# A graph layer, causal attention and eight experts on one core: pools split, roots and denominators moved, one branch at the end

## The chip, the core and the metric

The kernel runs on one core of one Trainium2 chip. A core has a matrix engine (PE), a vector engine (DVE), a scalar engine (ACT), a general engine (POOL, or GpSimd) and a queue engine for transfers (SP). Matmul results go to PSUM, eight banks of 2 KB a partition, from which DVE and ACT read them; the rest lies in SBUF. Each engine takes its instructions in the order in which they were written; across engines they wait on semaphores. The metric is the device time of one launch in microseconds, lower is better. Two kernels that differ by more than 0.2% can be told apart by several runs.

## What is computed

The input is 4096 tokens of 256 numbers and a 4096 x 4096 adjacency matrix, all in 32-bit floats. Cut to what matters:

```python
# layer 0: graph part
f = layernorm(x)
h = adj @ (f @ neigh_W.T) / (adj.sum(1) + 1)
x = x + concat([f, h]) @ lin_W.T
# attention and experts, on y = layernorm(x)
h = rmsnorm(y);  q, k, v = h @ wq.T, h @ wk.T, h @ wv.T     # 4 query heads, 2 key heads of 64
q, k = rope(q), rope(k)
att = softmax(causal(q @ k.T / 8));  z = y + (att @ v) @ wo.T
t = rmsnorm(z);  probs = softmax(t @ router_w.T)             # 8 experts, the best 2 are kept
out = z + sum over the two experts of weight * (silu(t @ w1.T) * (t @ w3.T)) @ w2.T
x = x + out
```

## The kernel before, in words

A planner is not used: instructions go to each engine in the order of the Python text. The line numbers are those of the kernel before.

**Graph part.** Tokens lie in 8 blocks of 512, and the adjacency matrix in 8 x 8 blocks. `aggregate(b, steps)` forms one block row: for each `jb` it multiplies by a seven-product (Strassen) scheme, line 412, 28 matmuls in all, each of which the profile records twice; after the seventh of 14 pairs it calls the steps that belong to that `jb` (lines 419 to 421). The sums that the scheme needs are made by `halve(n)` on DVE, four additions (lines 366 to 369), one of them into `kT`. `halve` of the next block stands at the top of each round (line 401). Row 0 has as its steps `features` (matmuls `pf`, line 377; ACT copies, line 382; DVE additions, line 385; four subtractions for `g`, lines 389 to 392), `turned_x` (transposes on PE, line 312) and `normed_x` (statistics on DVE, inverse root on POOL, lines 158 and 159, normalizing on DVE, line 167). Rows 1 to 7 have `qkv(b-1)`: `norm` at `jb` 0, then transposes, projections (line 179) and rotation. At the end of a row, lines 432 to 448 combine the seven products on ACT and DVE, up to `deg` (lines 440 to 442). In PSUM the part has two banks for `tr`, two for `pj` and four for `acc`, these from one pool of four buffers.

**Attention.** Runs of four key tiles, `runs`, follow each other: blocks in the order 3, 0, 4, 1, 5, 2, 6, 7, two head pairs each. A run has its scores (line 537; PE), exponentials (line 542; ACT, into `pt`), sums over keys (line 560; DVE) and products with the values (line 572; PE). The scores use one pool of three buffers of two banks each, `a_sc`; products have one bank, and everything else shares one bank, `ms`. In step n the order is: sums of the first tiles of run n, scores of run n+1, place 2n, the other sums, products of run n, place 2n+1. A place is where one piece of other work is put: `normalize` (denominators: `dn`, lines 585 to 591, with a DVE reciprocal), the output projection, routing, the writes of the rows into the experts' lists, the last block's projections, and a check of the scores' size, `guard`. `at` hands out places, one piece that uses PE at each.

**Experts.** Groups of 256 or 128 rows of one expert: `load_rows`, `load13` and `load2` on SP, `prepare` (transposes, line 1057), `hidden` (line 1078), `combine` (products, line 1123; scaling by the gate on DVE, line 1134; an indirect transfer that adds rows to the output, line 1151, on POOL). The score buffers hold `hidden`'s results. `combine` of group k-1 follows `hidden` of group k.

**The end.** After the last group every engine loads `rest_flag` and branches (lines 1258 and 1259) past four groups that are rarely needed; then every engine loads `flag` and branches (lines 1812 and 1813) past a general kernel for scores that are too large. With these inputs neither is taken. A drain and a barrier follow (line 1884).

Of the kernel before, what the change touches and what calls it, by code (L numbers as in the profile page):

```python
# [1 line left out]

# [6 lines left out]
F32 = mybir.dt.float32  # L9
# [7 lines left out]
P = 128  # L17
# [48 lines left out]
def fast_kernel(  # L66
# [13 lines left out]
    cos: bass.AP,  # L80
    sin: bass.AP,
    out: bass.AP,
    flag: bass.AP,
):


    nc = tc.nc
# [124 lines left out]
    with (  # L212
# [2 lines left out]
        tc.tile_pool(name="gx", bufs=2) as gx,  # L215
        tc.tile_pool(name="g_tr", bufs=2, space=PSUM) as p_tr,
        tc.tile_pool(name="g_pj", bufs=2, space=PSUM) as p_pj,
        tc.tile_pool(name="g_acc", bufs=4, space=PSUM) as p_acc,
    ):
        blocks = {}  # L220

# [102 lines left out]

        inputs, turned = {}, {}

        def normed_x(b):
            stats(gx, b)
            power(rstd[b], mv[b][:, :, 1:2], 1.0, EPS_LN)
            inputs[b] = gx.tile([P, TB, C], F32, tag="f", name=f"f_{b}", bufs=1)  # L330
            for t in range(TB):
                normed(inputs[b][:, t, :], b, t, rstd[b][:, t])
            nc.gpsimd.memset(g[b][:, G22 : T1 + 1, :, HC : HC + 1], 1.0)

        def turned_x(b):
            turned[b] = qT[b % 4]
# [35 lines left out]
        def features(b):  # L372
            fT = turned.pop(b)
            for t in range(TB):
                pj = p_pj.tile([P, 512], F32, tag="pj", name=f"pf_{b}_{t}")
                for c in range(2):
                    nc.tensor.matmul(
                        pj, fT[:, c, t * P : (t + 1) * P], ml_sb[:, c, :],
                        start=(c == 0), stop=(c == 1),
                    )  # L380
                i = t // 2 * 2
                nc.scalar.copy(
                    g[b][:, i : i + 2, t % 2, 0:HC], pj[:, 0:C].rearrange("p (h c) -> p h c", h=2)
                )
                nc.vector.tensor_add(res[b][:, t, :], res[b][:, t, :], pj[:, C : 2 * C])
                if b == 0 and t == 1:
                    halve(0)
            part = [g[b][:, k, :, 0:HC] for k in range(7)]
            nc.vector.tensor_sub(part[T1], part[G12], part[G11])
            nc.vector.tensor_sub(part[T3], part[G22], part[G12])  # L390
            nc.vector.tensor_sub(part[T2], part[G22], part[T1])
            nc.vector.tensor_sub(part[T4], part[T2], part[G21])

        def aggregate(b, steps):

            acc = [
                [p_acc.tile([P, 512], F32, tag="acc", name=f"acc_{b}_{t}_{k}") for k in range(2)]
                for t in range(2)
            ]
            for jb in range(NB):  # L400
                halve(b * NB + jb + 1)
                m = halves_of.pop(b * NB + jb)
                order = [(p, t) for p in PRODUCTS for t in range(2)]
                if jb == 0 and b:
                    load_tables(b - 1)
                if jb == NB - 1 or b and jb == 0:
                    order = [(p, t) for t in range(2) for p in PRODUCTS]
                for i, ((number, left, right), t) in enumerate(order):
                    bank, at, w = AT[number]
                    for k in range(2):  # L410

                        nc.tensor.matmul(  # L412
                            acc[t][bank][:, at : at + w], m[left][:, k, t * P : (t + 1) * P],
                            g[jb][:, right, k, 0:w],
                            start=(jb == 0 and k == 0 and number in (1, 3)),
                            stop=(jb == NB - 1 and k == 1),
                            skip_group_check=True,
                        )
                    if i == 6:
                        for step in steps.get(jb, ()):  # L420
                            step()
                load(b * NB + jb + 3)
# [27 lines left out]
        def qkv(b):  # L450

            made = {}

            def norm():
                stats(gx, b)
                var = mv[b][:, :, 1:2]
                power(rstd[b], var, 1.0, EPS_LN)
                power(both[b], var, *BOTH)
                made["h0"] = gx.tile([P, TB, C], F32, tag="f", name=f"h0_{b}", bufs=1)
                for t in range(TB):  # L460
                    normed(made["h0"][:, t, :], b, t, both[b][:, t])
# [18 lines left out]
            def turn_heads(t):  # L480
# [1 line left out]
                heads(b, t, made.pop(t), tr)  # L482

            return {
                0: [norm], 2: [turn], 3: [lambda: rotate(0)], 4: [lambda: rotate(1)],
                5: [lambda: turn_heads(0), lambda: rotate(2)],
                6: [lambda: turn_heads(1), lambda: rotate(3)],
                7: [lambda: turn_heads(2), lambda: turn_heads(3)],
            }


        normed_x(0)
        fold()
        load(2)
        for b in range(6, NB):
            load_x(b)
        turned_x(0)
        normed_x(1)
        features(0)
        turned_x(1)  # L500
        normed_x(2)
        steps = {
            jb: [
                lambda f=f, b=jb + k: f(b)
                for f, k in ((features, 1), (turned_x, 2), (normed_x, 3)) if jb + k < NB
            ]
            for jb in range(NB)
        }
        steps[3].append(load_rest)
        aggregate(0, steps)  # L510
        for b in range(1, NB):
# [5 lines left out]
    with (  # L517
# [1 line left out]
        tc.tile_pool(name="ex", bufs=2) as ex,  # L519
        tc.tile_pool(name="sp", bufs=9) as sp,  # L520
        tc.tile_pool(name="ax", bufs=2) as ax,
        tc.tile_pool(name="a_sc", bufs=3, space=PSUM) as p_sc,
        tc.tile_pool(name="a_y", bufs=1, space=PSUM) as p_y,
        tc.tile_pool(name="a_ms", bufs=1, space=PSUM) as p_ms,
    ):
        probs, sums, accs, ys, flats, chosen, squares, picks = ({} for _ in range(8))
        puts = []

        def scores(b, p, s):
# [1 line left out]
            sb, i = divmod(s, TB)  # L531
            off = i * P if sb == b else 0
            w = 512 - off
            ps = p_sc.tile([P, 2, 512], F32, tag="sc", name=f"sc_{b}_{p}_{s}")
            for j in range(2):
                hd = slice(j * HD, (j + 1) * HD)
                nc.tensor.matmul(  # L537
# [314 lines left out]
            ]  # L852


        def guard():
            six = {}

# [6 lines left out]
            def second():  # L864
# [9 lines left out]
                most = ax.tile([1, 1], F32, tag="most", name="most", bufs=1)  # L874
                nc.vector.tensor_reduce(most, qk2.rearrange("o p j -> o (p j)"), AX.X, ALU.max)
                nc.vector.tensor_scalar(most, most, 64.0 * LIMIT * LIMIT, None, op0=ALU.is_le)
                nc.vector.tensor_copy(flag, most)

            return [first], [second]


        HALF = GR // P
# [26 lines left out]

        table = eg.tile([P, 2, NG], I32, name="table")  # L910
        pads_at = eg.tile([P, NE], I32, name="pads_at")

        rest_flag = eg.tile([1, 1], I32, name="rest_flag")
        mine = eg.tile([P, NG, NE], F32, name="mine")

        def make_table(b, whole, g0, n):
# [54 lines left out]
            if whole:  # L971
# [5 lines left out]
                    base[:, 0:NE], left, float(size), base[:, 0:NE], op0=ALU.mult, op1=ALU.add  # L977
                )
            else:
                nc.vector.tensor_scalar(  # L980
                    rest_flag, ends[0:1, NE - 1 : NE], float(n - RARE), None, op0=ALU.is_gt
                )

        def entry(t, most):
            return nc.values_load(
# [82 lines left out]
        def hidden(k, step=None, behind=None):  # L1068
# [3 lines left out]
            hT = ex.tile([P, NF, n], F32, tag="hT", name=f"hT_{i}")  # L1072

            for q in range(0, NF + 1, 2):
                ps = p_sc.tile([P, 2, 2, GR], F32, tag="sc", name=f"h_{i}_{q}")[:, :, :, 0:n]
                for m in range(2 * q, min(2 * q + 4, 2 * NF + 1)):
                    for c in range(2):
                        nc.tensor.matmul(  # L1078
# [21 lines left out]
        def combine(k):  # L1100
# [10 lines left out]
            nc.vector.tensor_reduce(gt, pick, AX.X, ALU.add)  # L1111
            y = ax.tile([P, HALF, C], F32, tag="yT1", name=f"y_{i}")

            last = k == NM - 1
            ps = [
                pool.tile([P, HALF, C], F32, tag=tag, name=f"ye_{i}_{tag}")
                for pool, tag in ((p_y, "y"), (p_ms, "ms"))[: n if last else 1]
            ]

            def products(h):  # L1120
# [10 lines left out]
            for h in range(n):  # L1131
# [3 lines left out]
                    y[:, h, :], ps[h if last else 0][:, h, :], gt[:, h], None, op0=ALU.mult  # L1135
                )
                at = bass.IndirectOffsetOnAxis(ap=r[:, h, C : C + 1].bitcast(I32), axis=0)
                if k >= NM:
                    inside = dict(bounds_check=N - 1, oob_is_err=False)
                    was = y[:, 1, :]  # L1140
                    nc.vector.memset(was, 0.0)
                    nc.gpsimd.indirect_dma_start(
                        out=was, out_offset=None, in_=out[:, :], in_offset=at, **inside
                    )
                    nc.vector.tensor_add(y[:, h, :], y[:, h, :], was)
                    nc.gpsimd.indirect_dma_start(
                        out=out[:, :], out_offset=at, in_=y[:, h, :], in_offset=None, **inside
                    )
                    continue
                nc.gpsimd.memset(gap, 0.0)  # L1150
                put = nc.gpsimd.indirect_dma_start(  # L1151
                    out=(acc_dram if k < NM - LAST else out)[:, :],
# [47 lines left out]
        ends = {}  # L1200
        for n, (b, p, s) in enumerate(runs[:-1]):
            if s == TB * b:
                ends[b, p] = at(2 * n + 2, [[lambda b=b, p=p: normalize(b, p)]])
                taken.add(ends[b, p])
        at(0, last_qkv())
        end = 0
# [48 lines left out]
            if k + 2 < NM:  # L1255
                load2(k + 2)
        combine(NM - 1)
        more_rows = nc.values_load(rest_flag, min_val=0, max_val=1)
        with tc.If(more_rows != 0):
            for k in range(NM, NG):  # L1260
                load_rows(k)
                load13(k)
                load2(k)
                prepare(k)
                hidden(k)
                combine(k)
    kv_scope.close()

# [535 lines left out]
@with_exitstack  # L1806
def adj_ffn_kernel(ctx: ExitStack, tc: tile.TileContext, *args):
    nc = tc.nc
    flags = ctx.enter_context(tc.tile_pool(name="flags", bufs=1))
    flag = flags.tile([1, 1], I32, name="flag")  # L1810
    fast_kernel(tc, *args, flag)
    within = nc.values_load(flag[0:1, 0:1], min_val=0, max_val=1)
    with tc.If(within == 0):
        general_kernel(tc, *args)


# [71 lines left out]
```

## Time and profile before

| | us |
|---|---|
| median of the runs (1649.32 to 1652.04) | 1651.15 |
| the profiled execution | 1650.03 |
| its span, first to last instruction | 1648.22 |
| PE busy in the span | 1605.7 |
| DVE / ACT / POOL busy | 928.4 / 457.4 / 408.1 |

By stages, in busy us:

| stage | span, us | PE | DVE | ACT | POOL |
|---|---|---|---|---|---|
| graph part | 0 to 547.7 | 531.9 | 331.7 | 59.1 | 84.0 |
| attention | 547.7 to 1118 | 559.2 | 452.0 | 292.5 | 194.8 |
| experts | 1118 to 1633.5 | 514.5 | 144.2 | 105.8 | 126.0 |
| after the last matmul | 1633.5 to 1648.2 | 0.0 | 0.5 | 0.0 | 3.3 |

Matmuls are pipelined and their ends are modelled, so that the time from one matmul's start to the next tells more than its duration. "PEclk" is the share of the full clock that PE was granted. A wait is listed as who waited for whom, with its total, how often, and the longest.

### The profile page before, as it was taken

Reading aid. Unit: us, or ns where it says so; the run is one execution under the profiler, and the core shown is the slowest. Engines: PE = TensorE matmul, PEld = TensorE weight load, DVE = VectorE, ACT = ScalarE, POOL = GpSimd, SP = SyncE. Lnnn points to the kernel's source line nnn. Section 1 sums busy time; section 2 is a strip of 40 time slices with the busy share of each in tenths; the row PEclk is TensorE's granted clock in tenths of the full one; section 3 lists DMA queues with packets and bytes.
Section 4 is the critical chain, followed back from the end, with each engine's and each line's share of the span. In section 5 each row is a group of like instructions: output and inputs, shape, how many; then the busy total and the mean of one; then the engine's idle time right before and its main releaser. Section 6 shows DMA issues by size and latency. Waiting matters only on the chain. (4 is left out here: it accounts for less than half of the span.)

```text
span 1648.2 us, 24780 instructions
## 1 busy us (share of the span) xinstructions
PE 1605.7 (97%) x9588; PEld 1158.4 (70%) x9588; DVE 928.4 (56%) x1910; ACT 457.4 (28%) x866; POOL 408.1 (25%) x604
## 2 busy tenths in 40 slices
PE   7999999999999999999999999999999999999996
PEld 5779998999999534344343434338888999999985
DVE  6656656655665578778877887793432222222221
ACT  2110100000000445555555455553211221221120
POOL 1001111112112221342445323512422222212212
PEclk9999999999999999999999999999999999999998
DMA  6224434433433000000101000076766777777764
GB/s 223 97 78 149 140 133 152 145 141 131 157 131 132 4 1 1 27 27 27 40 14 39 28 13 28 26 222 190 239 171 200 220 253 247 220 240 251 243 208 102
DMA packets 67714, 209.76 MB, mean 127 GB/s; under 512 B 14656, under 2 KB 46272, under 8 KB 53952
## 3 DMA queue, kind: packets, MB, share of 16 engines
q1 hardware_dynamic: 54320, 190.05, 33.3%
q0 software_dynamic: 12720, 17.47, 5.6%
q8 instruction: 79, 1.29, 0.3%
q10 hardware_dynamic: 544, 0.52, 0.1%
q14 instruction: 51, 0.42, 0.1%
HBM read 180.81 MB, written 31.42 MB: 129 GB/s over the span
## 5 line engine op out<-in xcount | busy, mean ns | idle before, releaser
L542 ACT ACTIVATE pt<-sc 128x1024 f32<-128x1024 f32 (+3 forms) x288 | 251.8, 957 | 222.5 <-PE sc L537 167.8
L560 DVE TENSOR_TENSOR sum<-sum,pt 128x1024 f32<-128x1024 f32 (+3 forms) x258 | 295.2, 1144 | 18.9 <-POOL pt L544 0.3
L537 PE MATMUL sc<-qT_all,kT 64*128 64x512 f32 (+3 forms) x1152 | 253.5, 574 | 6.0 <-DVE deg L441 3.8
L412 PE MATMUL acc<-g,a 128*128 128x128 f32 x2048 | 255.7, 275 | 0.0
L572 PE MATMUL ya<-pt,vv 128*64 128x512 f32 (+3 forms) x1152 | 242.8, 563 | 0.0
L412 PEld LDWEIGHTS acc<-g,a 128*128 128x128 f32 x2048 | 241.8, 192 | 0.0
L1078 PE MATMUL h<-xT,qT_all 128*128 128x256 f32 (+1 forms) x1232 | 220.5, 335 | 0.0
L1085 DVE TENSOR_TENSOR hT<-si,h 128x256 f32<-128x256 f32 (+2 forms) x126 | 64.1, 509 | 262.1 <-ACT si L1084 262.1
L1078 PEld LDWEIGHTS h<-xT,qT_all 128*128 128x128 f32 x1232 | 194.2, 191 | 18.9 <-issue 1.0
L537 PEld LDWEIGHTS sc<-qT_all,kT 64*128 64x128 f32 x1152 | 104.5, 187 | 141.1 <-issue 109.2
L572 PEld LDWEIGHTS ya<-pt,vv 128*64 128x64 f32 x1152 | 78.0, 137 | 146.1 <-issue 140.1
L1151 POOL DMA_INDIRECT acc_dram<-y,rows x61 | 96.1, 1576 | 332.3 <-DVE y L1134 327.9
L1084 ACT ACTIVATE si<-h 128x256 f32<-128x256 f32 (+2 forms) x126 | 57.2, 454 | 376.0 <-PE h L1078 371.2
L1078 PE MATMUL h<-xT,res_all 128*128 128x256 f32 (+1 forms) x616 | 114.6, 342 | 0.0
L1078 PEld LDWEIGHTS h<-xT,res_all 128*128 128x128 f32 x616 | 100.3, 191 | 10.2 <-issue 0.2
L1123 PE MATMUL ye_y<-res_all,hT 128*128 128x256 f32 x440 | 102.3, 379 | 1.0 <-DVE y L1134 1.0
L412 PE MATMUL acc<-g,more_sums 128*128 128x129 f32 (+1 forms) x768 | 101.6, 274 | 0.0
L764 POOL DMA_INDIRECT lists<-row,slots x64 | 73.0, 1140 | 112.2 <-issue 109.4
L412 PEld LDWEIGHTS acc<-g,more_sums 128*128 128x128 f32 x768 | 94.6, 192 | 6.7 <-issue 6.7
L1123 PEld LDWEIGHTS ye_y<-res_all,hT 128*128 128x128 f32 x440 | 82.7, 190 | 12.1 <-DVE y L1134 1.4
L1134 DVE TENSOR_SCALAR y<-ye_y,gt 128x256 f32<-128x256 f32 x66 | 29.7, 480 | 87.6 <-PE ye_y L1123 87.5
L193 POOL TENSOR_TENSOR ro<-ro,r 128x192 f32<-128x192 f32 x28 | 16.5, 589 | 236.5 <-DVE r L190 236.5
(227 smaller groups left out, 1764.0 us busy)
## 6 DMA issues: line engine op xcount, KB each, us to landing
a<-in_adj_dram SPq DMA_DIRECT2D x64, 1024.0 KB, 4.8
qT_all<-in_w_dram SPq DMA_DIRECT2D x28, 1408.0 KB, 8.1
res_all<-in_w_dram SPq DMA_DIRECT2D x28, 768.0 KB, 5.1
res_all<-in_w_dram SPq DMA_DIRECT2D x14, 1408.0 KB, 7.7
qT_all<-in_w_dram SPq DMA_DIRECT2D x14, 768.0 KB, 5.4
rows<-lists SPq DMA_DIRECT2D x25, 265.0 KB, 3.0
lists<-pad SPq DMA_DIRECT2D x8, 662.5 KB, 13.7
res_all<-in_x_dram SPq DMA_DIRECT2D x8, 512.0 KB, 8.5
```

The lines of the kernel that those rows point to most:

```text
L412: nc.tensor.matmul(acc[t][bank][:, at : at + w], m[left][:, k, t * P : (t + 1) * P], g[jb][:, right, k, 0:w], start=(jb == 0 and k == 0 an ...
L537: nc.tensor.matmul(ps[:, j, :w], kT[sb][hd, i * P : (i + 1) * P], qT[b][hd, p, off:], start=True, stop=True,)
L542: nc.scalar.activation(pt[:, :, :w], ps[:, :, :w], AF.Exp, scale=HD ** -0.5)
L560: nc.vector.tensor_add(sums[b, p][:, :, off:], before[:, :, off:], pt[:, :, : 512 - off])
L572: nc.tensor.matmul(accs[b, p][hd, off:], vv[sb][:, i, hd], pt[:, j, : 512 - off], start=(s == 0), stop=(s == TB * b + TB - 1),)
L764: put = nc.gpsimd.indirect_dma_start(out=lists[:, :], out_offset=bass.IndirectOffsetOnAxis(ap=chosen[b][:, k, t, :], axis=0), in_=flats[b] ...
L1078: nc.tensor.matmul(ps[:, m % 2, m // 2 - q, :], w13_sb[:, c, m * P : (m + 1) * P], xT[:, c, :], start=(c == 0), stop=(c == 1),)
L1084: nc.scalar.activation(si[:, 0:both, :], ps[:, 0, 0:both, :], AF.Silu)
L1085: nc.vector.tensor_mul(hT[:, q : q + both, :], si[:, 0:both, :], ps[:, 1, 0:both, :])
L1123: nc.tensor.matmul(ps[h if last else 0][:, h, :], hT[:, q, cols] if q < NF else tail[:, cols], w2_sb[:, q, :], start=(q == 0), stop=(q == NF),
L1134: nc.vector.tensor_scalar(y[:, h, :], ps[h if last else 0][:, h, :], gt[:, h], None, op0=ALU.mult)
L1151: put = nc.gpsimd.indirect_dma_start(out=(acc_dram if k < NM - LAST else out)[:, :], out_offset=at, in_=y[:, h, :], in_offset=None, comput ...
```

## The change

Seven parts. The graph part's `acc` gets two pools of two buffers, and the scores three pools of one buffer each, taken in turn. In row 0, statistics and root (`scales_x`) are parted from the normalizing (`normed_x`), which now goes tile by tile between the additions of `features`, for the block after; `halve` follows `features` and `turned_x`. In `qkv`, statistics and both roots stay at `jb` 0, the one that is used first now ahead of the other, and the normalizing goes to `jb` 1. Denominators go from place 2n+2 to place 2n+3, and with them what is put after them. `guard` has an empty place between its two halves. The last two groups' products use two banks. The flag for large scores and the flag for rarely needed groups become one number, `left_over`, and one branch; the rare groups get a function of their own behind it.

```diff
-        tc.tile_pool(name="g_acc", bufs=4, space=PSUM) as p_acc,
+        tc.tile_pool(name="g_acc0", bufs=2, space=PSUM) as p_acc0,
+        tc.tile_pool(name="g_acc1", bufs=2, space=PSUM) as p_acc1,
...
-        def normed_x(b):
+        def scales_x(b):
             stats(gx, b)
             power(rstd[b], mv[b][:, :, 1:2], 1.0, EPS_LN)
-            inputs[b] = gx.tile([P, TB, C], F32, tag="f", name=f"f_{b}", bufs=1)
-            for t in range(TB):
-                normed(inputs[b][:, t, :], b, t, rstd[b][:, t])
             nc.gpsimd.memset(g[b][:, G22 : T1 + 1, :, HC : HC + 1], 1.0)
+
+        def normed_x(b, t):
+            if t == 0:
+                inputs[b] = gx.tile([P, TB, C], F32, tag="f", name=f"f_{b}", bufs=1)
+            normed(inputs[b][:, t, :], b, t, rstd[b][:, t])
...
                 nc.vector.tensor_add(res[b][:, t, :], res[b][:, t, :], pj[:, C : 2 * C])
+                if b + 1 < NB:
+                    normed_x(b + 1, t)
                 if b == 0 and t == 1:
                     halve(0)
...
             for jb in range(NB):
-                halve(b * NB + jb + 1)
+                if b:
+                    halve(b * NB + jb + 1)
...
-            def norm():
+            def scales():
                 stats(gx, b)
                 var = mv[b][:, :, 1:2]
+                power(both[b], var, *BOTH)
                 power(rstd[b], var, 1.0, EPS_LN)
-                power(both[b], var, *BOTH)
+
+            def norm():
                 made["h0"] = gx.tile([P, TB, C], F32, tag="f", name=f"h0_{b}", bufs=1)
...
-                0: [norm], 2: [turn], 3: [lambda: rotate(0)], 4: [lambda: rotate(1)],
+                0: [scales], 1: [norm], 2: [turn], 3: [lambda: rotate(0)], 4: [lambda: rotate(1)],
...
+        for jb in range(NB):
+            for f, b in ((features, jb + 1), (turned_x, jb + 2), (halve, jb + 1), (scales_x, jb + 3)):
+                if b < NB or f is halve:
+                    steps[jb].append(lambda f=f, b=b: f(b))
...
-        tc.tile_pool(name="a_sc", bufs=3, space=PSUM) as p_sc,
+        tc.tile_pool(name="a_sc0", bufs=1, space=PSUM) as p_sc0,
+        tc.tile_pool(name="a_sc1", bufs=1, space=PSUM) as p_sc1,
+        tc.tile_pool(name="a_sc2", bufs=1, space=PSUM) as p_sc2,
...
+        p_sc = cycle((p_sc0, p_sc1, p_sc2))
...
-            return [first], [second]
+            return [first], [None], [second]
...
+                nc.vector.tensor_max(rest, rest, too_large)
+                nc.vector.tensor_copy(left_over, rest)
+                nc.vector.tensor_copy(rare_table, table[:, :, NM:NG])
+                nc.vector.tensor_copy(rare_mine, mine[:, NM:NG, :])
...
-            last = k == NM - 1
+            last = k >= NM - 2
             ps = [
                 pool.tile([P, HALF, C], F32, tag=tag, name=f"ye_{i}_{tag}")
-                for pool, tag in ((p_y, "y"), (p_ms, "ms"))[: n if last else 1]
+                for pool, tag in ((p_ms, "ms"), (p_y, "y"))[0 if last else 1 :]
             ]
...
-                ends[b, p] = at(2 * n + 2, [[lambda b=b, p=p: normalize(b, p)]])
+                ends[b, p] = at(2 * n + 3, [[lambda b=b, p=p: normalize(b, p)]])
...
-        more_rows = nc.values_load(rest_flag, min_val=0, max_val=1)
-        with tc.If(more_rows != 0):
-            for k in range(NM, NG):
-                load_rows(k)
...
+def rare_groups(
...
+    for i in range(RARE):
+        at = entry(table[0:1, 0, i : i + 1], NE * REG)
+        r = sb.tile([P, ROW], F32, tag="r", name=f"y_rows_{i}")
+        nc.sync.dma_start(r, lists[bass.ds(at, P), :])
...
-    within = nc.values_load(flag[0:1, 0:1], min_val=0, max_val=1)
-    with tc.If(within == 0):
-        general_kernel(tc, *args)
+    state = nc.values_load(left_over[0:1, 0:1], min_val=0, max_val=2)
+    with tc.If(state != 0):
+        with tc.If(state == 2):
+            general_kernel(tc, *args)
+        with tc.If(state == 1):
+            ln2, w13, w2, out = (args[i] for i in (8, 9, 10, 13))
+            rare_groups(tc, ln2, w13, w2, out, lists, table, mine)
```

## The prediction

> **What bounds the kernel now.** First the page's totals, then PE's waits, then the stretches around the two longest, then lines in order of time.
>
> ```profile
> span 1648.2 us, 24780 instructions
> PE 1605.7 (97%) x9588; PEld 1158.4 (70%) x9588; DVE 928.4 (56%) x1910; ACT 457.4 (28%) x866; POOL 408.1 (25%) x604
> ```
>
> PE is idle for 42.5 us in all, 6.8 of them before the first matmul and 14.7 after the last. No engine is close behind. So whatever the change brings can come only from PE's holes, from its clock, and from the tail. The list of waits names the holes (total, how often, longest):
>
> ```profile
> PE acc L412 <- DVE kT L368: 6.3, 6, 1.0
> PE sc L537 <- DVE deg L441: 3.8, 1, 3.8
> PE dn L585 <- DVE sum L560: 2.9, 1, 2.9
> PE pf L377 <- DVE res_all L385: 2.5, 1, 2.5
> PE tn L866 <- DVE top L862: 1.2, 1, 1.2
> PE ye_y L1123 <- DVE y L1134: 1.0, 1, 1.0
> PE dn L585 <- DVE counts L724: 0.8, 1, 0.8
> ```
>
> The stretches show, after PE's, DVE's, ACT's and POOL's busy time, the granted clock:
>
> ```profile
> 547.00:560.00 13.00, 9.16 (x39) 4.66 (x37) 9.47 (x31) 6.18 (x8) 3.10 (x12) 0.87 0.04 12
> 865.00:880.00 15.00, 12.03 (x52) 4.85 (x49) 14.30 (x22) 5.99 (x8) 10.68 (x15) 0.89 0.18 63
> ```
>
> Both hold one of the long waits, and both lost clock: 13 x 0.13 = 1.7 us and 15 x 0.11 = 1.65 us of full-speed time. All other stretches between are at 1.00.
>
> **The change, part by part.** A wait is counted from the modelled end of the matmul before it (L412: 275 ns), which its successor normally doesn't await (24 of them took 2.84 us, so 0.11 us from start to start). Each wait removed is thus worth 0.16 us more than its row.
>
> *Score pools.* In the built order of the kernel before, the first scores wait for the last reader of `acc`, although their banks were `tr`'s. In the changed one, the first waits for the last `trq` copies (L209, ended at 545.4), the second for a projection read at 539, the third for `deg` of the first half (548.2). PE is free at 547.7 and reaches the third tile after two of 0.92 us each, at 549.4. So the wait goes whole: 3.8 + 0.16, and 1.7 of clock: 5.7. What is late next: DVE doesn't get ahead, its `deg` work ends at 552.6 as before, so the last block's statistics and roots keep their time while PE's transposes of `h_l` (567.56) come 5.7 us sooner, at 561.9. By the rows (sum 1.2, statistics 1.8, two roots on POOL 4.7, normalizing 1.4, with POOL at its slow readings) `h_l` is whole at 561.7. That fits, closely; if it fails, 1 us.
>
> *Roots, rows 1 to 7.* Here the order of time shows the stall:
>
> ```profile
> 196.47 2.84 PE L412 MATMUL acc<-g,a 128*128 128x128 f32 x24
> 200.36 1.16 PE L412 MATMUL acc<-g,kT 128*128 128x129 f32 x8 [1.04 <-DVE kT L368]
> ...
> 196.81 1.38 DVE L167 TENSOR_SCALAR h<-res_all,mv,both 128x256 f32<-128x256 f32 x4 [2.78 <-POOL both L159]
> 198.10 0.68 DVE L366 TENSOR_TENSOR qT_all<-a 128x512 f32<-128x512 f32 x1
> ```
>
> DVE waits 2.78 us for the second root, normalizes for 1.3, and only then makes the sums for `jb` 2. With the normalizing one round later the sums start after the statistics, at 194.05: 4 us earlier, where 1.04 are missing. Six times 1.04 + 0.16: 7.3. POOL's queue keeps its four instructions, in another order; nobody awaits `rstd` soon.
>
> *Row 0.* Here the change adds waits. Now the normalizing of the next block's tile t stands behind the addition of tile t, and the transposes follow at once:
>
> ```profile
> 39.19 7.03 PE L377 MATMUL pf<-qT_all 128*128 128x512 f32 x16
> 46.06 1.04 PE L312 MATMUL tr<-ident,f 128*128 128x128 f32 x8
> 46.26 0.38 ACT L382 COPY g<-pf 128x256 f32<-128x256 f32 x1 [1.34 <-PE pf L377]
> 46.67 0.42 DVE L385 TENSOR_TENSOR res_all<-res_all,pf 128x256 f32<-128x256 f32 x1 [1.30 <-ACT g L382]
> 47.01 0.42 DVE L389 TENSOR_TENSOR g<-g 128x256 f32<-128x256 f32 x1
> ```
>
> The last tile's normalizing takes the place of L389: 47.01 to 47.42. Its two transposes stand at 46.06 + 6 x 0.11 = 46.7: a stall of 0.74 in PE's queue, for blocks 2 to 7: 6 x 0.74 = 4.4. Behind them wait the other half of the products. For block 1, DVE has the first `halve` (2.65 us) between its tiles 1 and 2, so its transposes end 1.15 us later than now. At `jb` 7 `halve` comes behind the `g` subtractions (118.67): its third sum ends 2.15 us later, at 120.8, and PE wants it at 120.06: 0.75. Against this, additions of `features(1)` no longer stand behind `halve` and a normalizing that waits for POOL: the wait of 2.5 goes. Net: 4.4 + 1.15 + 0.75 - 2.5 - 0.16 = 3.65 lost. The bounds: 0 if DVE overlaps what I chain, 6.3 if nothing of the 2.5 is won.
>
> *Denominators a place on, and the gap in `guard`.* At 866.4 PE wants `dn`, and DVE, busy without a hole since 847, has 15 small instructions of routing and four sums ahead of it. One place on, PE first does a run's products (3.6 us), and the routing moves behind the four sums (2.95): the sum is ready at 866.9, `dn` is asked for at about 870. The wait goes: 2.9 + 0.16 + 1.65 of clock = 4.7. The wait on `counts` (0.8): two sums (2.45) now stand ahead of it, but `dn` comes 3.6 later: gone, 0.9. `tn2` has a place between: 1.2 + 0.16 = 1.4. Behind each `dn` on DVE waits the reciprocal (3.36) and behind that the next sums; DVE already waits 31 us for `dn` (8 of 16), so it has room. A transpose for routing now falls ahead of a narrow run at one more place, as it does at 664 and 718, where PE waited 0.64 for ACT: 0.6 lost. The first loads of the experts' weights start one place later, some 2.5 us, with rows first used 30 us after their issue (1083.75 to 1113.55): nothing; uncovered, those 2.5.
>
> *The last two groups.* POOL's queue sets the end:
>
> ```profile
> 1620.09 1.57 POOL L1151 DMA_INDIRECT out_dram<-y,rows  x1 [0.19 <-issue]
> ...
> 1627.92 1.57 POOL L1151 DMA_INDIRECT out_dram<-y,rows  x1 [6.14 <-DVE y L1134]
> ...
> 1629.79 1.57 POOL L1151 DMA_INDIRECT out_dram<-y,rows  x1 [0.19 <-issue]
> ...
> 1634.33 1.57 POOL L1151 DMA_INDIRECT out_dram<-y,rows  x1 [2.85 <-DVE y L1134]
> ```
>
> A group's puts wait for the landing of those before (3.8 us). With two banks the first half of the last but one is scaled at 1624.6 rather than 1627.15, so its second put takes the first one's time, 1627.92: the rest follows 1.9 earlier. PE's own 1.0 lies beside it and adds nothing.
>
> *One branch.* From the rows of line 1813 on POOL's queue (shortest/median/longest in ns, start of the first and the last):
>
> ```profile
> L1813 POOLq COMPARE_BRANCH  x1: 45/45/45, 1641.7 to 1641.7; - x1
> L1813 POOLq EVENT_SEMAPHORE  x1: 17/17/17, 1644.2 to 1644.2; - x1
> ```
>
> A load of the flag (0.31) comes before this branch, and 2.5 us pass after it until the target's first instruction. Both stand behind the last landing. The single branch is POOL's former first one, issued while the puts still land (4.9 us before the landing), which covers its jump; uncovered it would cost 2.5 again. So 2.9 go. The four DVE instructions for `left_over` fall where DVE is 28% busy: nothing.
>
> [...]
>
> Sum: 5.7 + 7.3 + 4.7 + 0.9 + 1.4 + 1.9 + 2.9 = 24.8 won, 3.65 + 0.6 = 4.25 lost, net 20.5. The profiled execution took 1650.0, so 1629.5. The median of the runs is 1.1 above it: 1630.6.
>
> **The rivals.**
> - *The waits in attention come back elsewhere.* `dn`, `counts` and places share one bank, and all moved together; a hole like 866 then opens at another block. For it: DVE is up to 38 of 41 us busy in some stretches. Against it: DVE's work ahead shrank as worked out. Price: the 4.7 + 0.9, so 1636.2.
> - *Row 0 costs nothing.* If transposes don't queue behind the additions, 3.65 come back: 1627. Against it: their wait on the last normalizing is in the built order.
> - *The boundary isn't cleared* (the change doesn't do what it says): another reader of those banks, or `h_l` late, holds PE: 5.7 stay, 1636.3.
> - *Slower: the denominators hold the one bank.* `dn` keeps it until the reciprocal ends. The next user comes 1.08 + 3.70 + 3.65 = 8.4 after it, so DVE may begin the reciprocal 4.0 us after `dn` ends. All 20.5 are lost once each of 16 denominators is 4.0 + 1.3 = 5.3 late; at 6.3 late it is 2.3 each, 36.8 in all: 1630.6 + 36.8 = 1667. With clock loss of 1.7 at half of them, 1681. Against it: the latest reciprocal now starts 2.0 us after its `dn` (750.9 to 752.84).
>
> **How the numbers follow.** As worked out 0.55 (own range 1627 to 1634); waits back 0.17; boundary 0.08; row 0 free 0.13; slower 0.05; small gains all lost, 0.02. The likeliest gives 1630.6. Cases of 1624 to 1641 hold eight in ten and more: below, row 0 free and small holes closed besides; above, two of the price-bearing rivals together. About 0.2% (3.3 us) is what a measurement tells from no change. Faster 0.93, same 0.02, slower 0.05.
>
> **What would show it.** Right: no wait of `acc` on `kT` in rows 2 to 7; scores start within 0.2 us of the last `acc`; PEclk at 1.00 from 10 to 1630; six new PE waits of some 0.7 at `tr` before 100 us; one branch of POOL before the last landing, and some 8 us from landing to end become 5. Wrong: a clock of 0.5 anywhere in attention, a `dn` wait over 2 us, or `tr` waits over 1.5 us each.

## The result, and the profile after

The changed kernel takes 1638.14 us (median of 6 runs, 1637.87 to 1638.98), against 1651.6 (6 runs, 1649.32 to 1652.88): a ratio of 0.992, 95% interval 0.9907 to 0.9933. That is faster, by 13.5 us; 1630.6 was forecast, 20.5 less than the 1651.15 of the first three runs. The profiled execution took 1638.25, its span is 11.7 shorter than that of before:

```profile
span 1636.5 us, 24754 instructions
PE 1603.5 (98%) x9588; PEld 1157.6 (71%) x9588; DVE 928.8 (57%) x1914; ACT 457.9 (28%) x866; POOL 405.0 (25%) x604
```

PE's waits in the changed kernel (total, how often, longest), all but the one for the first load and one of 0.2:

```profile
PE sc L555 <- ACT pt L560: 5.3, 4, 3.3
PE tr L318 <- DVE f L172: 4.4, 8, 0.7
PE po L624 <- DVE row L628: 1.7, 2, 1.0
PE po L624 <- DVE rden L608: 1.4, 1, 1.4
PE acc L423 <- DVE more_sums L376: 0.6, 1, 0.6
```

Every wait that the change was to remove is gone: `acc` on `kT`, `dn`, `pf` on `res_all`, `tn`, `ye_y`. The second line and the last are the forecast's row 0. In the first line the wait of 3.3 was not forecast; of its other three, of 0.64 each, two stood in the kernel before as well (at 665 and 719), and the one at 777.7 is the 0.6 that the forecast lost. The third and fourth lines were not in its sum; its rivals on attention had such waits. Where the time went is seen by following the same matmul through both traces (times in us from the start of the span):

| the first or last matmul of | before | after | gained up to here | in this stretch | forecast |
|---|---|---|---|---|---|
| row 1's first projection | 148.48 | 153.01 | -4.5 | -4.5 | -3.65 |
| the last `acc` | 547.47 | 544.05 | 3.4 | 7.9 | 7.3 |
| the first `tr_l` of the last block | 567.56 | 563.78 | 3.8 | 0.4 | 5.7 |
| the last `dn` | 1121.01 | 1113.56 | 7.5 | 3.7 | 6.4 |
| the last matmul of all | 1633.15 | 1624.46 | 8.7 | 1.2 | 1.9, see below |
| the end of the span | 1648.22 | 1636.52 | 11.7 | 3.0 | 2.9 |

Two rows fall short: the boundary between graph part and attention by 5.3, attention by 2.7. At the boundary the order of time in the changed kernel reads:

```profile
544.25 2.85 PE L555 MATMUL sc<-qT_all,kT 64*128 64x512 f32 x12
...
548.25 0.88 DVE L456 SCALAR_TENSOR_TENSOR res_all<-rows_sums,deg,res_all 128x256 f32<-128x256 f32 x2
...
549.36 2.85 ACT L560 ACTIVATE pt<-sc 128x1024 f32<-128x1024 f32 x3 [5.18 <-DVE res_all L456]
...
550.44 5.76 PE L555 MATMUL sc<-qT_all,kT 64*128 64x512 f32 x18 [3.34 <-ACT pt L560]
```

The scores do start at once, at 544.25. But three buffers of scores are then full, and ACT's first exponential doesn't begin before DVE's last addition of the graph part has ended, at 549.1. It writes `pt`, whose place in SBUF held `rows_sums` and `deg`, which that addition reads. The fourth tile waits for the first exponential. So PE's hole of 3.84 has become one of 3.34, three tiles later, and the clock goes with it again: it is at 0.5 from 550.35 to 553.76. In attention, in the middle of the three waits of the output projection:

```profile
865.15 1.03 PE L603 MATMUL dn<-sum,ones 128*64 128x512 f32 x4
865.40 1.22 DVE L578 TENSOR_TENSOR sum<-pt,pt 128x1024 f32<-128x1024 f32 x1
866.53 1.46 DVE L172 TENSOR_SCALAR row<-res_all,mv,rstd 128x256 f32<-128x256 f32 x4
867.91 2.56 DVE L578 TENSOR_TENSOR sum<-sum,pt 128x1024 f32<-128x1024 f32 x2
870.39 3.35 DVE L608 RECIPROCAL rden<-dn 128x512 f32<-128x512 f32 x1
...
873.79 1.99 PE L624 MATMUL po<-wo_sb,yT 128*128 128x256 f32 x8 [1.36 <-DVE rden L608]
```

`dn` itself has no wait any more. Its bank is free only when the reciprocal ends, and that stands behind three sums and four normalizing instructions: it starts 4.2 us after `dn` ended (866.2), and the next user of the bank, `po`, waits.

### The profile page after: what moved, and what is told of

Read it like the earlier page. It is cut to its first block, busy times and chain, and to the rows that moved or that the text cites. A ratio compares the mean times of both kernels' runs of the same rounds, so it can differ in the third digit from the quotient of the medians.

```text
span 1636.5 us, 24754 instructions
## 1 busy us (share of the span) xinstructions
PE 1603.5 (98%) x9588; PEld 1157.6 (71%) x9588; DVE 928.8 (57%) x1914; ACT 457.9 (28%) x866; POOL 405.0 (25%) x604
## 4 chain that ended last, share of the span: by engine, by line
PE 88%; DVE 6%; issue 2%; ACT 2%; POOL 1%; DMA 1%; DVEq 0%; SPq 0%; ACTq 0%; POOLq 0%
PE acc L423 24%; PE h L1105 20%; PE ya L590 11%; PE sc L555 11%; PE ye_y L1150 10%; PE pf L385 3%; PE pq L184 3%; DVE sum L578 3%; PE po L624 2%; ACT pt L560 1%; PE tx L1083 1%; PE dn L603 1%; PE tr L318 1%; PE trq L212 1%; PE pq_l L184 0%
## 5 line engine op out<-in xcount | busy, mean ns | idle before, releaser
L1105 PEld LDWEIGHTS h<-xT,res_all 128*128 128x128 f32 x616 | 100.3, 191 | 10.2 <-issue 0.2
L782 POOL DMA_INDIRECT lists<-row,slots x64 | 69.1, 1080 | 109.1 <-issue 106.5
L423 PE MATMUL acc<-g,qT_all 128*128 128x128 f32 (+1 forms) x512 | 74.0, 274 | 0.0
```

The costliest lines, as they stand in the source:

```text
L423: nc.tensor.matmul(acc[t][bank][:, at : at + w], m[left][:, k, t * P : (t + 1) * P], g[jb][:, right, k, 0:w], start=(jb == 0 and k == 0 an ...
L782: put = nc.gpsimd.indirect_dma_start(out=lists[:, :], out_offset=bass.IndirectOffsetOnAxis(ap=chosen[b][:, k, t, :], axis=0), in_=flats[b] ...
L1105: nc.tensor.matmul(ps[:, m % 2, m // 2 - q, :], w13_sb[:, c, m * P : (m + 1) * P], xT[:, c, :], start=(c == 0), stop=(c == 1),)
```

## Experiments

Times are medians; the changed kernel's is 1638.14. No experiment leaves out part of the computation.

**The exponential's buffer.** The row sums of the last block's second half go to a tile that stays (the last block's part of `qT`, unused by then), and the degree numbers of all blocks to `both`.

```diff
-                deg = gx.tile([P, 2], F32, tag="deg", name=f"deg_{b}_{t}")
+                if t and b == NB - 1:
+                    rows = qT[b][:, 0].rearrange("p (r h c) -> p r h c", r=2, h=2)
+                deg = both[b][:, 2 * t : 2 * t + 2, 0]
```

> The changed kernel with the last block's second half of row sums and its degree numbers in tiles that stay, so that the first exponential's buffer no longer lies where they lay. Theory A (the stall at the boundary moved from the scores' banks to the exponential's buffer, which waits for DVE's last addition): ACT's first exponential starts at about 545.5 instead of 549.36, PE's hole of 3.34 before the fourth tile goes, the clock stays at 1.00 there (1.7 us): 5.2 us less, of which up to 1.0 may come back at the last block's transposes, since the root they need is the second on POOL: 1633 to 1634. Rival B (DVE's own work for the last block, or the banks, holds the scores whatever the buffer): 1637 to 1639, with the hole at another tile.

Measured: 1633.45 (1632.86 to 1634.59), 4.7 less. In the order of time, and in the stretch (PE's busy time first, granted clock behind the five engines):

```profile
544.16 7.17 PE L557 MATMUL sc<-qT_all,kT 64*128 64x512 f32 x32
...
545.46 7.44 ACT L562 ACTIVATE pt<-sc 128x1024 f32<-128x1024 f32 x8 [1.38 <-PE sc L557]
```

```profile
540.00:557.00 17.00, 17.00 (x96) 9.02 (x97) 11.87 (x37) 9.84 (x16) 5.94 (x14) 1.00 0.03 9
```

PE has no hole and no clock loss; the first exponential is 3.9 earlier. The last block's normalizing ends at 557.9, its transposes begin at 558.48: they didn't wait. Theory A holds.

The same edit alone in the kernel before:

> The kernel before with the same edit alone. Theory A: nothing, 1651 plus or minus 1.5, since there the scores wait for their banks until 551.58 and the exponential's wait ended (552.55) about when the first tile was there: two waits side by side, of which one alone is worth nothing. Rival B2 (the buffer was the costlier one all along): 3 us less or more, 1648.

Measured: 1651.37, ratio 0.9993 (0.9983 to 1.0003) to before. Nothing, as A says. The rows of the kernel before at this place:

```profile
551.58 5.83 PE L537 MATMUL sc<-qT_all,kT 64*128 64x512 f32 x18 [3.84 <-DVE deg L441]
551.67 0.88 DVE L445 SCALAR_TENSOR_TENSOR res_all<-rows_sums,deg,res_all 128x256 f32<-128x256 f32 x2
...
552.87 1.02 ACT L542 ACTIVATE pt<-sc 128x1024 f32<-128x1024 f32 x1 [5.28 <-PE sc L537]
```

There the two waits lay side by side: the banks held PE until 551.58, and the addition that frees the buffer ended at 552.55, about when PE's first tile was there for ACT. Either one taken away alone left the other.

**The scores in one pool again**, the row products still in two:

```diff
-        tc.tile_pool(name="a_sc0", bufs=1, space=PSUM) as p_sc0,
-        tc.tile_pool(name="a_sc1", bufs=1, space=PSUM) as p_sc1,
-        tc.tile_pool(name="a_sc2", bufs=1, space=PSUM) as p_sc2,
+        tc.tile_pool(name="a_sc", bufs=3, space=PSUM) as p_sc0,
...
-        p_sc = cycle((p_sc0, p_sc1, p_sc2))
+        p_sc = cycle((p_sc0,))
```

> The changed kernel with the scores in one pool of three buffers again (the row products stay in their two pools). Theory A (parting the scores' pool lets them start 3.9 us earlier, but the fourth tile waits for the first exponential all the same, so that the parting alone is worth 0.4): one hole of 3.8 to 4.0 ahead of the first tile, clock lost once, 1638.1 to 1639. Rival B (the early start is worth more than the drift of 0.36 shows): 1640 or more.

Measured: 1638.77 (1638.43 to 1639.02), 0.6 more. The size is A's, but the hole isn't where I put it: the first tile waits 0.4 for `deg`, the fourth 2.9 for ACT. So long as the buffer of `pt` waits, parting the scores' pool is worth half a microsecond at most; the ratios to the kernel before, 0.9925 (0.9911 to 0.994) here and 0.992 (0.9907 to 0.9933) in the changed kernel, don't tell it from nothing.

**Row 0.** All four tiles of a block are normalized ahead of the additions (block 1's ahead of the first `features`), and the sums stand at the top of the round but for the first round.

```diff
-                if b + 1 < NB:
-                    normed_x(b + 1, t)
...
-                if b:
+                if b or jb:
                     halve(b * NB + jb + 1)
...
-            for f, b in ((features, jb + 1), (turned_x, jb + 2), (halve, jb + 1), (scales_x, jb + 3)):
-                if b < NB or f is halve:
+            for f, b in (
+                (normed_x, jb + 2), (features, jb + 1), (turned_x, jb + 2), (halve, jb + 1),
+                (scales_x, jb + 3),
+            ):
+                if b < NB if f is not halve else jb == 0:
```

> The changed kernel with row 0 in another order: all four tiles of a block are normalized ahead of the additions of the block before it, and the sums for the next step stand at the top of the round, but for the first round. Theory A (PE's six waits of 0.75, the 1.23 at block 1 and the 0.8 at jb 7 come from DVE's order alone): all gone, 6.5 less: 1631.6. Rival B (additions behind four more instructions and the sums come late): waits of the products for the additions as in the kernel before, 2.5 at one block or more: 1634 to 1638.

Measured: 1631.51 (1630.12 to 1633.19), 6.6 less. PE's waits in that kernel, all but the one for the first load:

```profile
PE sc L556 <- ACT pt L561: 5.3, 4, 3.3
PE po L625 <- DVE row L629: 1.7, 2, 1.0
PE po L625 <- DVE rden L609: 1.4, 1, 1.4
PE pf L385 <- DVE res_all L393: 0.5, 1, 0.5
```

`tr` and `acc` are gone from the list. Theory A holds; of B's wait, 0.5 turned up. Part of the 6.6 may be the clock: the two shorter of the four executions (1630.12 and 1630.36) show a mean clock of 0.998, the two longer 0.997 and 0.995. The profiled execution, which lost the clock once at the boundary like that of the changed kernel, has a span 5.6 shorter.

**The same hole before.** In the kernel before, only the first round's sums go behind the additions of block 1.

```diff
-                halve(b * NB + jb + 1)
+                if b or jb:
+                    halve(b * NB + jb + 1)
...
+        steps[0].insert(2, lambda: halve(1))
```

> The kernel before with one thing moved: in the first round of row 0 the sums for the next step stand behind the additions of block 1 instead of ahead of them. Theory A (the wait of 2.5 near 25.5 us also costs the clock in most executions, 1.7 us of full-speed time, though not in the profiled one, so that the median holds one loss more than that profile): 2.6 + 1.7 less, 1647.5 to 1648, the mean clock 0.995 in nearly all executions. Rival B (the clock falls only behind holes of 2.9 or more, and the median's distance from that profile is something else): 2.6 less, 1649 to 1649.5, with executions at 0.994 as often as before.

Measured: 1651.82, ratio 1.0004 (0.9995 to 1.0013). Neither theory. The wait of `pf` for `res_all` is still there with 2.0, now until 42.7 us, one block later: there the sums at the top of the round and the normalizing behind its root stand ahead of the additions, as they did at 25 us in the kernel before. Taking `halve` away from one block alone only hands the stall on, so this run says nothing on the clock.

**Denominators back at place 2n+2:**

```diff
-                ends[b, p] = at(2 * n + 3, [[lambda b=b, p=p: normalize(b, p)]])
+                ends[b, p] = at(2 * n + 2, [[lambda b=b, p=p: normalize(b, p)]])
```

> The changed kernel with the denominators back at place 2n+2. Theory A (the move won its 2.9 us wait, 1.65 of clock and the 0.8 on counts, and gave back some 2.8 as waits of the output projection): the wait of dn near 866 is back at 2.5 to 3.0, the clock falls to 0.5 behind it, the projection's waits are under 0.5 together: 1640 to 1641.5. Rival B (the wait only changes its place, and the move was worth nothing): 1637.5 to 1639.

Measured: 1640.46 (1640.02 to 1640.93), 2.3 more. The waits of `dn` are back, 2.9 and 0.8, and the clock at 0.5 from 865.04 to 868.45; those of `po` are gone from the list. Theory A holds: the move is worth 2.3, not the 5.6 of the forecast.

**Rows normalized earlier**, away from the reciprocals at 750 and 870:

```diff
-            end = at(max(ends[b, 1] + 1, end - 4), after(b))
+            start = max(ends[b, 1] + 1, end - 4)
+            first, *others = after(b)
+            at(start - 8, [first])
+            end = at(start, [[None], *others])
```

> The changed kernel with the normalizing of a block's rows (four DVE instructions, 1.4 us, in the stretch ahead of the reciprocals at 750 and 870) eight places earlier. Theory A (the three waits of the output projection for DVE, 0.8, 1.5 and 1.2 us from start to start, are DVE's backlog, of which 1.4 us are these four): 2 to 3 less, 1635 to 1636, with those waits under 0.3 together. Rival B (DVE's backlog is older than eight places, or the reciprocal of 3.35 us holds the one bank by itself): the waits stay or turn up elsewhere, 1637 to 1639.

Measured: 1637.58 (1637.35 to 1637.9), 0.6 less. Two of the three waits are gone (1.4 became 0.2, the one near 764 went), the third, `po` on `row` (near 880 in the changed kernel), stays at 1.1. The ratio, 0.9911 (0.9894 to 0.9927), is hardly told from the changed kernel's; the waits show what went. PE's last matmul comes 1.5 earlier, the end only 1.0, since a put's landing took 4.8 us where it took 4.5. So A is right for two waits, B for the third: there DVE is behind by more than those 1.4.

**Two branches in place of one.** The rare groups and the general kernel each get a load of `left_over` and a branch of their own.

```diff
-    with tc.If(state != 0):
-        with tc.If(state == 2):
-            general_kernel(tc, *args)
-        with tc.If(state == 1):
-            ln2, w13, w2, out = (args[i] for i in (8, 9, 10, 13))
-            rare_groups(tc, ln2, w13, w2, out, lists, table, mine)
+    with tc.If(state == 1):
+        ln2, w13, w2, out = (args[i] for i in (8, 9, 10, 13))
+        rare_groups(tc, ln2, w13, w2, out, lists, table, mine)
+    state = nc.values_load(left_over[0:1, 0:1], min_val=0, max_val=2)
+    with tc.If(state == 2):
+        general_kernel(tc, *args)
```

> The changed kernel with two loads of the number and two branches in place of one, one behind the other: first past the rare groups, then past the general kernel. Theory A (a branch that stands behind the last landing costs its jump of some 2.5 us and a load of 0.3): 2.5 to 3.0 more, 1640.6 to 1641.2, all of it between the last put and the end. [...]

Measured: 1642.44 (1641.61 to 1643.38), 4.3 more. The second branch's rows on POOL's queue (shortest/median/longest in ns, start of the first and the last):

```profile
L1919 POOLq COMPARE_BRANCH  x1: 45/45/45, 1634.1 to 1634.1; - x1
L1919 POOLq EVENT_SEMAPHORE  x1: 17/17/17, 1636.6 to 1636.6; - x1
```

Again 2.5 us lie between the branch and its target, behind the last landing. From that landing to the end it is 8.0 us, against 5.0 in the changed kernel and 8.0 in the one before: 3.0, as A says. Not every branch has this jump: the first branch of this run, past the rare groups alone, has 0.8 from branch to target on POOL and 0.4 on ACT (0.5 on ACT at the first branch of the kernel before), where the single branch of the changed kernel, past both, has 2.6 and 2.5. The remaining 1.1 of this span is puts that landed later: one took 5.1 us where it took 4.5, and the next waits for it.

**Two banks for the last group alone:**

```diff
-            last = k >= NM - 2
+            last = k >= NM - 1
```

> The changed kernel with two banks for the last group alone, whose first half now takes the other bank than the group before it. Theory A (of this part only PE's wait of 1.0 for the bank was ever worth anything, since the last group's puts wait for its own halves and a landing, and the wait goes by the order of the banks alone): 1637.8 to 1638.8, no wait of ye. Rival B (the forecast's: an earlier second put of the last but one group is what counts): 1639.5 to 1640.2.

Measured: 1639.76 (1638.81 to 1640.36), 1.6 more: rival B, my forecast's own reasoning, against the theory that I had formed from the table above. POOL's puts in the changed kernel:

```profile
1617.87 1.57 POOL L1166 DMA_INDIRECT out_dram<-y,rows  x1 [3.77 <-DVE y L1161]
...
1620.46 1.57 POOL L1166 DMA_INDIRECT out_dram<-y,rows  x1 [0.91 <-DVE gt L1138]
...
1625.66 1.57 POOL L1166 DMA_INDIRECT out_dram<-y,rows  x1 [3.52 <-DVE y L1161]
```

and in this one, where PE has no wait for the bank either:

```profile
1620.23 1.57 POOL L1166 DMA_INDIRECT out_dram<-y,rows  x1 [6.20 <-DVE y L1161]
...
1622.10 1.57 POOL L1166 DMA_INDIRECT out_dram<-y,rows  x1 [0.19 <-issue]
...
1626.60 1.57 POOL L1166 DMA_INDIRECT out_dram<-y,rows  x1 [2.81 <-DMA out_dram<-y,rows]
```

The second put is 1.6 earlier with two banks, and the third, the last group's first, waits for its landing. The row of the changed kernel names DVE's scaling, but there too the third put starts 0.74 after that landing (at 1624.92, 4.45 after the second put's start; in this run at 1625.86, 3.75 after). To take away PE's wait alone wins nothing: from the last `h` to the end it takes 24.1 here, 22.4 in the changed kernel, and 23.7 in the kernel before without the 3.0 of its second branch.

**All three gains together**, with the last block's two roots in the other order besides:

```diff
-                power(rstd[b], var, 1.0, EPS_LN)
                 power(both[b], var, *BOTH)
+                power(rstd[b], var, 1.0, EPS_LN)
```

> The changed kernel with the edits of x1_kept, x2_row0 and x3_early together, and the last block's two roots in the other order. If the three gains are independent they add: 4.7 + 6.6 + 0.6 to 1.4 of 1638.1 give 1625.4 to 1626.2, the clock at 1.00 from 13 to 1610 us, and PE's waits the one of 1.1 for the output projection, three of 0.65 for ACT and little else. If part of them was one stall seen twice: 1628 or more.

Measured: 1626.54 (1625.55 to 1626.83), ratio 0.9851 (0.9836 to 0.9866) to the kernel before, 11.6 less than the changed kernel. The three alone gave 4.7 + 6.6 + 0.6 = 11.9: they add, to within 0.3. In the spans of the profiled executions, where the clock losses are known, it is 4.6 + 5.6 + 1.0 = 11.2 against 12.0, so a part of the close agreement is luck. The other order of the two roots was not run alone. PE's waits behind its first load:

```profile
PE sc L558 <- ACT pt L563: 1.9, 3, 0.6
PE po L627 <- DVE row L631: 1.1, 1, 1.1
PE pf L385 <- DVE res_all L393: 0.5, 1, 0.5
PE dn L606 <- DVE six L891: 0.4, 1, 0.4
PE po L627 <- DVE rden L611: 0.2, 1, 0.2
```

The clock is at 1.00 from 12.2 to 1616.5 without a break. This version beats both kernels.

**ACT's squares a place later**, on top of that:

```diff
-            for t in range(2 * h, 2 * h + 2):
+            for t in range(TB if h else 0):
```

> The kernel x7_all with ACT's squares of a block's first half moved from the first transposing place to the second. Theory A (the three waits of 0.65 of narrow scores for ACT come from the two squares that stand ahead of the exponentials, 1.2 us on ACT): up to 2.4 less than x7_all, 1624.1 to 1625. Rival B (the four squares then stand ahead of the next run's exponentials, and the wait moves there): 1626 to 1627.

Measured: 1626.12 (1625.67 to 1627.1), against 1626.54: no difference that can be told. Two of the three waits went, but the one that ended near 766 grew from 0.64 to 1.7, and one of 1.1 opened that ended near 948. The last matmul starts at 1612.33 and 1612.34.

## Why the forecast was right in direction, and a third of its gain did not come

The time lies within the forecast's range, but the case "as worked out" didn't come about. What came is two of its rivals at once, the boundary that isn't cleared (8%) and waits in attention that come back elsewhere (17%), the second of them at about half its price. Most of its signs came (the scores' start, the six waits of `tr`, the end), but not the clock at 1.00 throughout, and one sign of being wrong did: a clock of 0.5 in attention, at 550.35. Point by point, by its steps:

- *Score pools, 5.7 forecast, 0.4 measured.* This is the step that failed. The first two tiles' readers, the start of the scores and the bound from `h_l` were right: the scores started at 544.25, and with the buffer freed the transposes of `h_l` fitted as computed. What failed is "what is late next". I followed DVE to the last block's statistics, but not ACT, the reader of the scores. That its first write into SBUF waits for the graph part's last DVE instruction was in the built order of both kernels, and hidden in the one before behind PE's wait. The rival had the price (5.7) and the wrong cause (another reader of the banks, or `h_l`).
- *Roots, rows 1 to 7, 7.3 forecast, 7.9 measured.* Right: no wait of `acc` on `kT` in rows 2 to 7, and each of the six rows is 1.31 shorter where I counted 1.2.
- *Row 0, 3.65 lost, 4.5 measured.* Right, down to the six waits of 0.75 from start to start, 1.2 at block 1 and 0.8 at `jb` 7. The rest, 0.6, stands at the very start and is no cost of the change: the first matmul of `features` begins at 11.99, against 11.42, but in two other profiles, of kernels that have the code of the kernel before up to there, it begins at 11.87 and 12.04. That this loss is DVE's order alone is shown by the run without it, so that the rival "row 0 costs nothing" was open to another order, not to this one.
- *Denominators and `guard`, 6.4 forecast, 3.7 measured.* The waits of `dn`, `counts` and `tn` went, and so did the clock loss near 870. (PE wanted `dn` at 867.0, where the scores ahead of it end, and not at 866.4; the wait of 2.9 is counted from there, so nothing in the sum changes.) The term that failed is the cover for what was moved: "DVE already waits 31 us for `dn`, so it has room". That is a sum over eight places, and the room isn't at the two where DVE is behind. My slower rival had the right mechanism and even its threshold, a reciprocal that begins over 4.0 us after `dn` ends; it was passed at one place (4.2) and cost 1.4 there, where the rival asked for all sixteen.
- *The last two groups, 1.9 forecast.* Mis-sized: 1.2 by the trace, 1.6 by the run with one bank for the last but one group. The landing that the last group waits for took 4.5 us in place of 3.8 us, which takes 0.65 off. It took 4.2 to 5.1 in all nine profiles with two banks for both groups, and 3.8 to 4.3 in the four others, so it may belong to the change; why it is longer isn't shown. That PE's own 1.0 adds nothing was right, and I doubted it wrongly afterwards.
- *One branch, 2.9 forecast, 3.0 measured.* Right: on POOL's queue three profiles show 2.5 to 2.6 us from the branch past the general kernel to its target (2.5 in the kernel before, 2.6 in the changed one, 2.5 with two branches).
- *The median 1.1 above the profile.* Wrong: it is 0.1 below. See the last section for the likeliest cause.

## What to carry to other kernels

When a wait at a stage boundary is removed, look in the built order for the next engine's first write as well: the pools that took over memory of the stage before carried waits of their own here, in SBUF (PE's 3.34 us in the changed kernel) as in PSUM (its 3.84 in the kernel before), and either one taken away alone left the other. A move that relieves one engine is to be checked at the place where the other is furthest behind, not against its idle time in all. And a stall inside a chain of additions may only be handed to the next block, as the 2.5 us near 25 us became 2.0 near 42; read where it reappears before booking the gain.

## What was not expected of the hardware

In these profiles PE's clock fell by the windows of a grid, not by the length of a hole alone. In all of them the stretches at 0.5 between the first and the last matmul last 3.413 us, or twice that, and start whole multiples of 3.413 us after the first rise of the clock (159 and 252 of them in the kernel before, 158 in the changed one). Cut along that grid, two executions of nearly the same code differ; first the kernel before, near 25 us and at the boundary (stretch, its length, PE's busy time, then the other engines and the granted clock):

```profile
23.54:26.95 3.41, 2.53 (x6) 0.76 (x4) 2.77 (x7) 0.75 (x2) 0.59 (x2) 1.00 0.24 77
26.95:30.37 3.42, 1.84 (x5) 0.89 (x6) 1.85 (x4) 0.00 (x0) 0.00 (x0) 1.00 0.02 5
30.37:33.78 3.41, 3.41 (x21) 2.40 (x20) 1.49 (x4) 1.82 (x4) 0.00 (x0) 1.00 0.00 0
...
549.19:552.61 3.42, 1.03 (x6) 0.65 (x8) 3.01 (x12) 0.00 (x0) 0.00 (x0) 1.00 0.02 5
552.61:556.02 3.41, 3.41 (x12) 1.62 (x10) 0.53 (x1) 2.05 (x2) 1.58 (x10) 0.50 0.12 40
```

then the kernel before with the exponential's buffer freed, whose hole near 26 us is the same 2.5:

```profile
26.29:29.70 3.41, 0.96 (x3) 0.30 (x2) 3.17 (x6) 0.37 (x1) 0.00 (x0) 1.00 0.00 0
29.70:33.12 3.42, 3.42 (x5) 1.35 (x4) 0.05 (x1) 0.37 (x1) 0.00 (x0) 0.50 0.02 5
```

In the first execution the hole is split over two windows, 0.9 and 1.6 idle, and costs nothing more; in the second it falls into one window, 2.5 idle, and the next window is at 0.50. Counted over thirteen profiles (windows at full clock, between the first and the last matmul), each of the fifteen windows in which PE was idle for 2.05 us or more was followed by one at 0.5, and none with 1.75 or less was; between the two there was none. (In the kernel before it was 2.38 and 2.92 against at most 1.57, in the changed kernel 3.25 against at most 1.36.) In two profiles a second window at 0.5 followed the first; what decides that isn't shown. That a hole of 2.5 us falls into two windows in one execution and into one in another would explain why the kernel before spreads over 3.6 us and the changed one over 1.1, and why the medians differ by 1.7 more than the profiles: the profiled execution of before lost the clock twice, the other one above three times. That the third loss is in most executions wasn't shown by itself, since the run made for it moved the hole without removing it. The executions of the kernel before that were measured beside the experiments agree with it: of 41, 29 show a mean clock of 0.994 (the three losses give 0.994, the two 0.995) and have a median of 1652.24, 11 show 0.995 and have 1650.07, and one shows 0.997 and took 1646.88. The mean also holds the stretch at 0.5 behind the last matmul (10.2 us in the profile of before, 7.6 in that of the changed kernel), so that losses can't be counted from it with certainty.
